# A four-layer graph network on one core: f1's first rows stored and spread through other queues, the decoder's last product in two parts

## The chip, the cores and the metric

One core of one Trainium2 chip runs the whole program in one launch. The metric is the device time of a launch in microseconds; the kernel before was run four times. Profiled executions are recorded by the hardware profiler, which gives every instruction's start and duration on TensorE (PE, and PEld for its weight loads), VectorE (DVE), ScalarE (ACT), GpSimd (POOL) and SyncE (SP), and the DMA traffic by queue: q1 is fed by SP, q10 by ACT, q0 by GpSimd.

## The reference

Input are 2708 nodes with 512 features (x) and a 2708 x 2708 adjacency matrix of zeros and ones (adj, about 1.2% ones and the diagonal). Four layers follow, each as `x = layernorm(x + layer(x, adj))`:

```
layer 0:  Xw = x @ W (4 heads of 128);  f1 = Xw . v1,  f2 = Xw . v2
          att = softmax over the neighbours of sigmoid(f1[i] + f2[j])
          Xa = att @ Xw;  batchnorm;  emb = batchnorm(elu(Xn @ We.T + b) + Xn)
          Y = elu((att @ emb) @ W.T);  out = batchnorm(elu(Y @ Wd.T + b) + Y)
layer 1:  A @ (x @ W + b) / degree
layer 2:  adj * (softmax(x @ node_w) * softmax(masked (x Ew)(x Ew).T)) @ (x W) + b
layer 3:  softmax(q k.T / sqrt(512) + 2 adj) @ v
```

The change lies in layer 0: at its very start, where f1 is made, and at the end of its decoder (the last line of layer 0), where the statistics of the last batchnorm are completed.

## The kernel before

The 2708 nodes are cut into 22 row blocks of 128 (the last has 20 rows). Layer 0 works on two halves of the columns (1354 each, a half being three chunks of 452, 452 and 450) and two pairs of heads. Features lie on the partitions in "feature tiles" of 128 x 4 x 2708, called xT_sb, ft and ot in turn.

**The start (project, L219 to L323).** SP's queue loads x transposed in six chunks (L232), and in between the first two blocks of the adjacency (L241), small weights and the parameters (L243). PE makes f1 for a chunk (f1_rows, L263: four products of 32 rows each), DVE copies it to the tile `stage` (L270). After the three chunks of the first half, one DMA of 4 x 1354 floats stores f1 to DRAM (L275), and two DMAs read one head's row each and spread it to 128 partitions (L277): f1b[0] and f1b[1], 677 KB each. They are needed because f1 has to lie along the free axis on every partition. All three DMAs are issued by SP. Beside this, PE makes Xw and f2 for the 22 row blocks (values_of, L285, three PSUM tiles in turn), ACT copies Xw of the first 14 blocks to SBUF and DVE that of the others (L294), and DVE takes f2 (L298).

**The attention pass (attention_pass, form).** For each row block j, the adjacency block is loaded (L379, by SP), zeros become a large negative number (DVE, L395 and L396), and the block is stored to adj_d for later passes (L400, by GpSimd). ACT computes tanh(0.5 f1 + 0.5 f2) for both heads (L407, from f1b[0] and f1b[1]), DVE combines it with the mask (L415, 128 x 2708), ACT takes the exponential (L416), and PE adds the block's share to the output sums (L503, twelve records a block) and to the row sums (L540). Four tiles t and four tiles a are in flight. The loads of blocks 2 and 3 are ordered behind the second spread where that is an instruction of their own queue (issue_after, which orders instructions of one engine).

**What sets the order.** A scheduler writes one instruction order for each engine from the program's order, dependencies and its own estimates; an engine then runs its list in order. A DMA's wait stands in the list of the engine that issues it, so whatever is behind it on that engine waits too.

**The decoder's end (decode, from L862).** For the last pair of heads of the second half, three chunks q are taken in turn. For each chunk and each of four groups o of 128 features, mlp makes one product (L914, four matmuls of 128 x 128 weights with 452 or 450 columns, two records each), ACT the exponential (L558), DVE the two steps of the elu (L563, L565), the sum with the input (L938) and the batch statistics (L939, bn_stats). Of the last chunk's last group, o = 3, everything after it depends: bn_aggr (L575) over six partial statistics for each o, scale and shift (L107 to L109, L578, L585, L586), and then layer 1's input stage, in which ACT applies scale and shift (L1066), DVE adds x (L1073) and PE transposes (L1079) and multiplies with w1 (L128). Beside the tail, PE makes one small product for a later layer (L1020), ACT copies it (L1027), and SP stores it (L1028).

Of the kernel before, what the change touches and what calls it, by code (L numbers as in the profile page):

```python
# [29 lines left out]
def gnn_stack_kernel(  # L30
# [25 lines left out]
    nc = tc.nc  # L56
    N, F = x.shape
    H = w0.shape[1]
    C = F // P
# [75 lines left out]
    NHALF, HB, HP = 2, 3, 2  # L135
# [10 lines left out]
    SQ = 4  # L146
# [31 lines left out]
    with ExitStack() as l0:  # L178
# [8 lines left out]
        f1_d = dram.tile([H, N], F32, name="f1_d")  # L187
# [6 lines left out]
        def feat_tile(name):  # L194
            return pf.tile([P, C, N], F32, tag="feat", name=name)
# [23 lines left out]
        def project(att, psum):  # L219
# [39 lines left out]
            def f1_rows(ci, dst):  # L259
                c0, w = CHUNKS[ci]  # L260
                pf = psum.tile([P, BANK], F32, tag=f"psm{ci % 2}", name="pf")
                for h in range(H):
                    nc.tensor.matmul(  # L263
                        pf[32 * h : 32 * h + 32, :w],
                        wv1[:, h, :],
                        xT_sb[:, h, c0 : c0 + w],
                        start=True,
                        stop=True,
                    )
                nc.vector.tensor_copy(dst[:, :w], pf[:, :w])  # L270

            h0, w = HSPAN[0]
            for ci, (q0, _) in enumerate(HCH[0]):
                f1_rows(ci, stage[:, q0:])
            nc.sync.dma_start(f1_d[:, h0 : h0 + w], stage[0 : 32 * H : 32, :w])  # L275
            for k in range(HP):
                spread = nc.sync.dma_start(  # L277
                    f1b[k][:, :w], f1_d[k, h0 : h0 + w].partition_broadcast(P)
                )
            def values_of(jt):  # L280
# [287 lines left out]
        def stats_tile(name, k):  # L568
            return p0.tile([P, C, k, 6], F32, tag=name, name=name)

        def batch_scale(stats, gamma, name):

            mv = pf.tile([P, C, 2], F32, name=f"{name}_mv")
            for c in range(C):
                nc.vector.bn_aggr(mv[:, c, :], stats[:, c].rearrange("p k s -> p (k s)"))  # L575
            scale = pf.tile([P, C], F32, name=f"{name}_scale")
            inv_std(scale, mv[:, :, 1], BN_EPS)
            nc.vector.tensor_tensor(scale, scale, prm_sb[:, gamma, :], ALU.mult)  # L578
            return scale, mv[:, :, 0]
# [27 lines left out]
        stats = stats_tile("stats_a", SQ * NHALF)  # L607
        bias = p0.tile([P, 2, C], F32, name="enc_bias")
        with (
# [3 lines left out]
            f1b, blocks, spread, rest = project(att, psum)  # L613
# [84 lines left out]
            for name, w in (("wq", wq), ("wk", wk)):  # L698
                for part in range(2):
                    tag = "z" if len(raws) == 3 else "a"  # L700
                    t = att.tile([P, HW], F32, tag=tag, name=name, bufs=1 if tag == "z" else 4)
                    t = t[:, : half * F].rearrange("p (c o) -> p c o", c=half)
# [19 lines left out]
        with (  # L722
# [41 lines left out]
            stats = stats_tile("stats_b", NCH)  # L764
# [16 lines left out]
            for ci, (c0, w) in enumerate(CHUNKS):  # L781
# [15 lines left out]
                for o in range(C):  # L797
                    dst = ft[:, o, c0 : c0 + w]
                    r = elu(
                        att, pss[o][:, :w], w, bias[:, 0, o : o + 1], bias[:, 1, o : o + 1]  # L800
                    )
# [16 lines left out]


            ot = feat_tile("ot")  # L820
            stats = stats_tile("stats_c", NCH)
            dec_w = load_mlp(dec_wT, "dec_w")
            links = {}
            spare = []
# [37 lines left out]
            def decode(hf, p, po, rb):  # L862
                h0, w = HSPAN[hf]
# [8 lines left out]
                t = ot[:, :, h0 : h0 + w]  # L872
                last = p + 1 == H // HP
                final = last and hf == NHALF - 1
# [30 lines left out]
                    nc.tensor.matmul(ps[:, :qw], w0T_sb[:, h, :], y, start=True, stop=True)  # L905
                    elu(att, ps[:, :qw], qw, dst=y)

                def mlp(q, o, st, wide):


                    q0, qw = HCH[hf][q]
                    ps = psum.tile([P, BANK], F32, tag="misc", name="ps_dec", bufs=2)
                    for c in range(C):
                        last_dec[0] = nc.tensor.matmul(  # L914
                            ps[:, :qw],
                            dec_w[:, c, o * P : (o + 1) * P],
                            t[:, c, q0 : q0 + qw],
                            start=(c == 0),
                            stop=(c == C - 1),
                        )  # L920
                    r = None
                    if wide:
                        if o == 0:
                            st["r"] = att.tile([P, HP, HW], F32, tag="t", name="r_dec", bufs=4)
                        r = st["r"].rearrange("p k w -> p (k w)")[:, o * BW : o * BW + qw]
                    r = elu(
                        att,
                        ps[:, :qw],
                        qw,
                        prm_sb[:, MB_DEC, o : o + 1],  # L930
                        bm1[:, o : o + 1],
                        dst=r,
                        last=final and q + 1 == HB and o + 1 == C,
                    )
                    st.setdefault("sums", []).append((t[:, o, q0 : q0 + qw], r, o))

                    def add(dst, y, r, o):
                        nc.vector.tensor_tensor(dst, y, r, ALU.add)  # L938
                        nc.vector.bn_stats(stats[:, o, HB * hf + q, :], dst)  # L939

                    if wide and o + 1 < C:
                        y, r, o = st["sums"][-1]
                        add(r, y, r, o)
                    elif o + 1 == C:
                        for y, r, o in st["sums"]:
                            if wide and o + 1 < C:
                                nc.scalar.copy(y, r)
                            else:
                                add(y, y, r, o)

                def after(k, q):
                    shifted(k, q)
# [2 lines left out]
                if not final:  # L955
# [4 lines left out]
                    for q in range(HB if last else 0):  # L960
                        st = {}
                        wide = q + 1 == HB
# [25 lines left out]
                for q in range(HB):  # L988
                    st = {}
                    mlp(q, 0, st, True)  # L990
                    mlp(q, 1, st, True)
                    if q + 1 < HB:
                        turns(q + 1)
                    if q + 2 < HB:
                        begin(q + 2)
                    mlp(q, 2, st, True)
                    if q == 0:
                        centre(po[0])
                    mlp(q, 3, st, True)


                rest = [
# [32 lines left out]
        nc.vector.tensor_reduce(dsum, zeros, AX.X, ALU.add)  # L1035
        nc.vector.tensor_scalar(dsum, dsum, -1.0, float(N), ALU.mult, ALU.add)
        nc.vector.reciprocal(rdeg, dsum)
        scale3, mean3 = batch_scale(stats, MG_DEC, "bn3")
        shift3 = batch_shift(scale3, mean3, MBETA_DEC, "bn3")
        xs, w1_sb, x_held = held1["xs"], held1["w1"], held1["x"]  # L1040

# [2 lines left out]
    with (  # L1044
# [62 lines left out]
        for g in range(0, NT, G):  # L1107
            group = range(g, min(g + G, NT))
            c0 = g * P
            w = min(N, c0 + G * P) - c0  # L1110
# [35 lines left out]
            for it in group:  # L1146
                n = BLOCKS[it][1]
                y = xs[:n, it, :]
# [412 lines left out]
    with (  # L1561
# [61 lines left out]
    with (  # L1623
# [96 lines left out]
        def finish3(it, po, rs):  # L1720
# [23 lines left out]
            sums=lambda: room(13, 4, C, GW),  # L1744
# [9 lines left out]
        for t in range(start3 + steps + lag):  # L1754
# [87 lines left out]
```

## Time and profile before

| | us |
|---|---|
| median of four runs | 3234.18 (3232.56 to 3238.33) |
| the profiled execution's own time | 3238.33 |
| its span | 3236.6 |
| PE busy | 3200.6 (99%) |
| DVE busy | 1929.2 (60%) |
| ACT busy | 1318.8 (41%) |
| f1 rows ready on DVE (L270's third copy ends) | 19.12 |
| first spread, second spread issued by SP | 24.62, 24.96 |
| first tanh, second tanh start | 30.79, 33.48 |
| first L503 on PE | 44.08 |
| last product of the decoder ends on PE, about | 1152.9 |
| last bn_aggr ends on DVE | 1157.08 |
| first transpose of layer 1 on PE | 1159.23 |

The span is the time from the first to the last instruction of the profiled execution; a little of the launch lies around it. PE's busy time is modelled from the starts of pipelined matmuls, so it says where PE stands still, not how well it is used. A gap on PE is read with its "granted clock", the TensorE clock that was in force, as a share of full speed. In a timeline row the numbers are the start, the length, the engine, the line and what it writes and reads; the bracket at the end is the idle time of the engine before it, and who ended it.

### The profile page before, as it was taken

Reading aid. Unit: us, or ns where it says so; the run is one execution under the profiler, and the core shown is the slowest. Engines: PE = TensorE matmul, PEld = TensorE weight load, DVE = VectorE, ACT = ScalarE, POOL = GpSimd, SP = SyncE. Lnnn points to the kernel's source line nnn. Section 1 sums busy time; section 2 is a strip of 40 time slices with the busy share of each in tenths; the row PEclk is TensorE's granted clock in tenths of the full one; section 3 lists DMA queues with packets and bytes.
Section 4 is the critical chain, followed back from the end, with each engine's and each line's share of the span. In section 5 each row is a group of like instructions: output and inputs, shape, how many; then the busy total and the mean of one; then the engine's idle time right before and its main releaser. Section 6 shows DMA issues by size and latency. Waiting matters only on the chain.

```text
span 3236.6 us, 30335 instructions
## 1 busy us (share of the span) xinstructions
PE 3200.6 (99%) x10874; PEld 1716.2 (53%) x10874; DVE 1929.2 (60%) x3160; ACT 1318.8 (41%) x1498; POOL 136.3 (4%) x220
## 2 busy tenths in 40 slices
PE   8999999999999999999999999999999999999999
PEld 5444444544444446875555555554555555555554
DVE  7889987876686685444145677776344342542533
ACT  6898886467767451001143434442011020120211
POOL 1100100000000000000010000000000000000000
PEclk9999999999999999999999999999999999999999
DMA  8867865256555413540054444553211111111100
GB/s 281 313 221 265 290 236 188 71 170 231 189 172 187 166 57 116 144 115 1 1 147 121 130 128 137 149 160 98 75 41 34 43 35 38 43 30 46 34 24 20
DMA packets 175702, 400.35 MB, mean 124 GB/s; under 512 B 21275, under 2 KB 116455, under 8 KB 169215
## 3 DMA queue, kind: packets, MB, share of 16 engines
q1 hardware_dynamic: 158622, 315.64, 32.0%
q0 software_dynamic: 16496, 80.70, 6.5%
q8 instruction: 85, 1.39, 0.2%
q10 hardware_dynamic: 432, 2.08, 0.2%
q14 instruction: 67, 0.54, 0.0%
HBM read 315.46 MB, written 81.30 MB: 123 GB/s over the span
## 4 chain that ended last, share of the span: by engine, by line
PE 85%; issue 8%; DVE 3%; ACT 2%; DMA 1%; POOL 1%; SPq 0%; POOLq 0%; DVEq 0%; ACTq 0%
PE po L1407 24%; PE ps_s L1286 18%; PE po L503 16%; PE ps_nb L1139 7%; PE ps_wide L1188 5%; PE ps_sup L1584 2%; PE ps_hid L128 2%; PE ps_o L1515 2%; PE ps_dec L914 2%; PE ps_mlp L789 1%; PE psm L540 1%; PE ps_s L1278 1%; ACT t L416 1%; PE tp L1178 1%; DVE t L415 1%
## 5 line engine op out<-in xcount | busy, mean ns | idle before, releaser
L415 DVE SCALAR_TENSOR_TENSOR t<-t,a 128x2708 f32<-128x2708 f32 (+1 forms) x150 | 444.3, 2975 | 151.8 <-ACT t L407 147.7
L407 ACT ACTIVATE t<-f1b,f2h 128x1354 f32<-128x1354 f32 (+1 forms) x300 | 411.6, 1413 | 59.1 <-PE po L503 32.9
L503 PE MATMUL po<-t,xw 128*128 128x452 f32 (+3 forms) x1056 | 410.5, 552 | 4.2 <-ACT t L416 4.2
L1286 PE MATMUL ps_s<-sup,hT 128*128 128x384 f32 (+1 forms) x1176 | 407.4, 490 | 0.0
L1407 PE MATMUL po<-sup,e 128*128 128x512 f32 x882 | 407.0, 595 | 0.0
L1407 PE MATMUL po<-e,xs 128*128 128x384 f32 (+1 forms) x1176 | 406.0, 489 | 0.0
L416 ACT ACTIVATE t<-t 128x2708 f32<-128x2708 f32 (+1 forms) x150 | 367.9, 2454 | 90.7 <-DVE t L415 90.6
L503 PE MATMUL po<-t,emb 128*128 128x452 f32 (+3 forms) x1056 | 398.5, 546 | 3.8 <-ACT t L416 3.8
L1718 DVE SCALAR_TENSOR_TENSOR e<-a_cols,ps_s 128x384 f32<-128x384 f32 (+1 forms) x154 | 85.5, 555 | 449.9 <-PE ps_s L1286 427.0
L1286 PEld LDWEIGHTS ps_s<-sup,hT 128*128 128x128 f32 x1176 | 221.8, 190 | 164.2 <-issue 14.2
L1407 PEld LDWEIGHTS po<-e,xs 128*128 128x128 f32 x1176 | 222.2, 190 | 160.2 <-issue 5.8
L503 PEld LDWEIGHTS po<-t,xw 128*128 128x128 f32 (+1 forms) x1056 | 189.9, 191 | 213.8 <-issue 198.2
L503 PEld LDWEIGHTS po<-t,emb 128*128 128x128 f32 (+1 forms) x1056 | 194.2, 191 | 201.1 <-issue 193.2
L1407 PEld LDWEIGHTS po<-sup,e 128*128 128x128 f32 x882 | 160.4, 190 | 159.3 <-issue 137.1
L1286 PE MATMUL ps_s<-hT 128*128 128x384 f32 (+5 forms) x672 | 211.0, 461 | 0.9 <-ACT sup L1591 0.7
L1385 ACT ACTIVATE e<-e 128x384 f32<-128x384 f32 (+1 forms) x308 | 151.7, 522 | 117.4 <-DVE e L1384 114.6
L1139 PE MATMUL ps_nb<-hid_hi,at 128*128 128x512 f32 x484 | 185.4, 390 | 0.4 <-DVE at L1131 0.4
L1633 ACT ACTIVATE a_cols<-a_cols,neg_big 128x384 f32<-128x384 f32 (+1 forms) x154 | 94.6, 617 | 217.9 <-DMA a_cols<-in_adjT_dram 185.6
L1139 PE MATMUL ps_nb<-hid_lo,at 128*128 128x512 f32 x462 | 179.9, 389 | 0.0
L1384 DVE TENSOR_TENSOR e<-e,nmax 128x384 f32<-128x384 f32 (+1 forms) x308 | 162.6, 550 | 23.3 <-ACT nmax L1377 23.3
L108 ACT ACTIVATE ln_rstd<-ln_rstd 128x1 f32<-128x1 f32 (+1 forms) x88 | 17.3, 201 | 388.8 <-DVE ln_rstd L107 388.0
L1286 PEld LDWEIGHTS ps_s<-hT 128*128 128x128 f32 x672 | 123.2, 190 | 89.3 <-issue 19.6
(253 smaller groups left out, 3323.4 us busy)
## 6 DMA issues: line engine op xcount, KB each, us to landing
a<-adj_d SPq DMA_DIRECT2D x108, 677.0 KB
a_cols<-in_adjT_dram SPq DMA_DIRECT2D x378, 192.0 KB
kept<-t POOLq DMA_DIRECT2D x22, 1354.0 KB, 6.4
t<-kept SPq DMA_DIRECT2D x22, 1354.0 KB
a<-in_adjT_dram SPq DMA_DIRECT2D x42, 677.0 KB
adj_d<-a POOLq DMA_DIRECT2D x42, 677.0 KB, 6.1
raw<-in_adjT_dram SPq DMA_DIRECT2D x105, 256.0 KB
a_cols<-in_adjT_dram SPq DMA_DIRECT2D x63, 202.0 KB
```

Source lines behind the costliest of these rows:

```text
L407: tanh = nc.scalar.activation(tv[:, k, :], f1b[k][:n, :w], AF.Tanh, bias=f2h[:n, jt, h : h + 1], scale=0.5,)
L415: step = nc.vector.scalar_tensor_tensor(tv, tv, GUARD, ab, ALU.add, ALU.mult)
L416: exp = nc.scalar.activation(tv, tv, AF.Exp, scale=0.5)
L503: nc.tensor.matmul(po[HB * k + q][:, :qw], values[r : r + n, jt, h * P : (h + 1) * P], t[r : r + n, k, q0 : q0 + qw], start=(place == 0), ...
L1139: nc.tensor.matmul(pos[it][:n], at, half[:, jt, :], start=(jt == 0 and k == 0), stop=(jt == NT - 1),)
L1188: nc.tensor.matmul(ps[:, :width], w(c, o), xt(c), start=(c == 0), stop=(c == C - 1),)
L1286: nc.tensor.matmul(ps[:, b * P : w], keys[:, c, j0 : j0 + P], st["q"][:, c, b * P :], start=(c == 0), stop=(c == C - 1),)
L1384: nc.vector.tensor_tensor(e, e, st["nmax"][:, :w], ALU.add)
L1385: nc.scalar.activation(e, e, AF.Exp)
L1407: nc.tensor.matmul(out, lhsT, rhs, start=(k == 0), stop=(k == NT - 1))
L1633: nc.scalar.activation(a, a, AF.Identity, bias=neg_big[: a.shape[0]], scale=1.0e30)
L1718: nc.vector.scalar_tensor_tensor(e, a, 2.0, ps, ALU.mult, ALU.add)
```

## The change

Three edits. The store of f1's first rows is issued by ACT instead of SP. The spread of the second head's row is issued by GpSimd instead of SP. The last product of the decoder (last chunk, o = 3) is computed in two parts of 225 columns, each with its own exponential, elu, sum and statistics; the statistics tile has one more place for it (and takes the storage of an earlier one), and bn_aggr of o = 3 runs over seven places, of the others over six as before.

```diff
-            nc.sync.dma_start(f1_d[:, h0 : h0 + w], stage[0 : 32 * H : 32, :w])
+            nc.scalar.dma_start(f1_d[:, h0 : h0 + w], stage[0 : 32 * H : 32, :w])
             for k in range(HP):
-                spread = nc.sync.dma_start(
+                queue = nc.gpsimd if k else nc.sync
+                spread = queue.dma_start(
                     f1b[k][:, :w], f1_d[k, h0 : h0 + w].partition_broadcast(P)
                 )
...
-        def batch_scale(stats, gamma, name):
+        def batch_scale(stats, gamma, name, more=0):
...
             for c in range(C):
-                nc.vector.bn_aggr(mv[:, c, :], stats[:, c].rearrange("p k s -> p (k s)"))
+                k = stats.shape[2] - (more if c + 1 < C else 0)
+                nc.vector.bn_aggr(mv[:, c, :], stats[:, c, :k].rearrange("p k s -> p (k s)"))
...
-            stats = stats_tile("stats_c", NCH)
+            stats = stats_tile("stats_a", SQ * NHALF)[:, :, : NCH + 1]
...
-                def mlp(q, o, st, wide):
+                def mlp(q, o, st, wide, part=None):
                     q0, qw = HCH[hf][q]
+                    nth = HB * hf + q
+                    if part is not None:
+                        q0, qw, nth = q0 + part * (qw // 2), qw // 2, nth + part
+                    done = part in (None, 1)
...
-                        last=final and q + 1 == HB and o + 1 == C,
+                        last=final and q + 1 == HB and o + 1 == C and done,
...
-                    st.setdefault("sums", []).append((t[:, o, q0 : q0 + qw], r, o))
+                    st.setdefault("sums", []).append((t[:, o, q0 : q0 + qw], r, o, nth))
...
-                    if wide and o + 1 < C:
+                    if not done:
+                        y, r, o, nth = st["sums"].pop()
+                        add(y, y, r, o, nth)
+                    elif wide and o + 1 < C:
...
-                    mlp(q, 3, st, True)
+                    if q + 1 < HB:
+                        mlp(q, 3, st, True)
+                    else:
+                        mlp(q, 3, st, True, 0)
+                        mlp(q, 3, st, True, 1)
...
-        scale3, mean3 = batch_scale(stats, MG_DEC, "bn3")
+        scale3, mean3 = batch_scale(stats, MG_DEC, "bn3", more=1)
```

The engines' orders move with it. On ACT the store stands behind the fifth of the 14 copies of Xw. On GpSimd the second spread stands behind the first adj_d store. On DVE the mask step L395 of block 2 stands ahead of the first L415 (before, behind the copy of the last f1 chunk, L270), and some mask steps near the end of the first half change places with L415. At the decoder's end DVE interleaves the two parts of o = 3 with the steps of o = 2; on ACT the three copies of r_dec (L947) stand between the two exponentials, and the square root of the scale (L108) ahead of the copy L1027.

More of the change, by code (lines that the diff above doesn't have):

```diff
@@ L924, in mlp @@
                             st["r"] = att.tile([P, HP, HW], F32, tag="t", name="r_dec", bufs=4)
-                        r = st["r"].rearrange("p k w -> p (k w)")[:, o * BW : o * BW + qw]
+                        r = st["r"].rearrange("p k w -> p (k w)")
+                        r = r[:, o * BW + (part or 0) * qw :][:, :qw]
                     r = elu(
@@ L932, in mlp, with add @@
                         dst=r,
-                        last=final and q + 1 == HB and o + 1 == C,
+                        last=final and q + 1 == HB and o + 1 == C and done,
                     )
-                    st.setdefault("sums", []).append((t[:, o, q0 : q0 + qw], r, o))
-                    def add(dst, y, r, o):
+                    st.setdefault("sums", []).append((t[:, o, q0 : q0 + qw], r, o, nth))
+                    def add(dst, y, r, o, nth):
                         nc.vector.tensor_tensor(dst, y, r, ALU.add)
-                        nc.vector.bn_stats(stats[:, o, HB * hf + q, :], dst)
-                    if wide and o + 1 < C:
-                        y, r, o = st["sums"][-1]
-                        add(r, y, r, o)
+                        nc.vector.bn_stats(stats[:, o, nth, :], dst)
+                    if not done:
+                        y, r, o, nth = st["sums"].pop()
+                        add(y, y, r, o, nth)
+                    elif wide and o + 1 < C:
+                        y, r, o, nth = st["sums"][-1]
+                        add(r, y, r, o, nth)
                     elif o + 1 == C:
-                        for y, r, o in st["sums"]:
+                        for y, r, o, nth in st["sums"]:
                             if wide and o + 1 < C:
@@ L948, in mlp @@
                             else:
-                                add(y, y, r, o)
+                                add(y, y, r, o, nth)
                 def after(k, q):
```

## The prediction

> **What bounds the kernel now.** I read the page's summary first: PE is busy 99% of the span and is 85% of the chain that ended last, so an edit counts only where PE stands still or where something moves PE's start. The change touches two such places, the first 50 us and the end of the decoder, about 1150 to 1160 us. For the first I read the chain of waits over the first 60 us (start, length, what):
>
> ```profile
> 18.48 0.64 DVE f_rows L270
> ...
> 19.14 5.46 DMA f_d<-f_rows
> ...
> 25.01 8.45 DMA f1b<-f_d
> ...
> 33.48 1.43 ACT t L407
> ...
> 34.93 2.98 DVE t L415
> ...
> 38.73 2.09 PE pxw L285 x8
> ```
>
> The f1 rows are ready at 19.12, their store takes until 24.60, the two spreads until 33.48 (the first head's row lands at 30.79). The first mask step (L415) runs 34.93 to 37.91, and PE, which had run out of work at 35.54, waits until 38.73, because the copies that free its PSUM tiles (L294 on DVE) stand behind that step in DVE's order. The windows view shows what the wait costs beyond itself (after the window: busy us and count of PE, PEld, DVE, ACT, POOL, then granted clock, DMA share, GB/s):
>
> ```profile
> 36.00:38.00 2.00, 0.00 (x0) 0.00 (x0) 2.00 (x2) 1.58 (x3) 0.00 (x0) 0.99 0.76 311
> 38.00:40.00 2.00, 1.27 (x6) 1.30 (x7) 2.00 (x7) 2.00 (x1) 0.00 (x0) 0.50 0.52 84
> 40.00:42.00 2.00, 2.00 (x10) 1.42 (x10) 1.61 (x4) 2.00 (x3) 0.62 (x1) 0.50 0.68 274
> 42.00:44.00 2.00, 2.00 (x12) 0.55 (x9) 2.00 (x3) 1.04 (x1) 0.57 (x1) 0.50 0.05 9
> 44.00:46.00 2.00, 2.00 (x5) 1.07 (x5) 2.00 (x4) 0.87 (x1) 0.02 (x1) 0.81 0.20 44
> ```
>
> After the gap of 3.19 us the clock is 0.50 to about 45 us. The same view shows a second case: PE waits 3.31 us before 864.73 and has 0.50 until about 870. The third gap is the decoder's end, 2.79 us up to 1159.23, and there the clock stays:
>
> ```profile
> 1156.40:1159.30 2.90, 0.12 (x2) 0.08 (x2) 1.80 (x9) 1.75 (x5) 0.00 (x0) 1.00 0.63 175
> ```
>
> So between 2.79 and 3.19 us of idle lies a step, and the start is just past it. From 50.43 on PE starts a new row block every 6.03 us (50.43, 56.46, 62.48) without a gap, DVE needs 5.5 per block; what the start gains or loses, the end gains or loses.
>
> At the decoder's end the timeline shows DVE, not PE, as the last:
>
> ```profile
> 1153.98 0.69 DVE L563 TENSOR_SCALAR elu_r<-ps_dec,bm 128x450 f32<-128x450 f32 x1 [0.21 <-ACT elu_m L558]
> 1154.70 0.63 DVE L565 SCALAR_TENSOR_TENSOR r_dec<-elu_m,elu_r 128x450 f32<-128x450 f32 x1
> 1155.43 0.63 DVE L938 TENSOR_TENSOR ot<-ot,r_dec 128x450 f32<-128x450 f32 x1
> 1156.10 0.63 DVE L939 BATCH_NORM_STATS2 stats_c<-ot 128x6 f32<-128x450 f32 x1
> 1156.76 0.32 DVE L575 BATCH_NORM_AGGREGATE bn_mv<-stats_c 128x2 f32<-128x36 f32 x1
> ```
>
> The 0.21 is DVE's only wait since 1150.75; scale and shift follow, and PE's first transpose comes at 1159.23.
>
> **The store on ScalarE's queue.** SP's queue holds 7 MB of loads ahead of the store; the DMA share is 0.9 or more until 24 us. On ACT the store stands behind the fifth of the 14 copies of xw (19.10 to 19.69), so it starts 0.55 later than SP's, costs 0.35 of ACT (the L453 issues take 326 to 348 ns), and nine copies and then the tanh steps are queued behind it. ACT idles 0.31 before each of these copies, which hides it; without that cover it is 0.35 on the PSUM copies. Landing: the nearest rows are the three 7 KB stores to the same tensor from GpSimd's queue, 1.7, 3.2 and 4.9 us. From 19.69 that is 21.4 to 24.6; I take the middle, 22.9. The first spread on SP then starts 1.7 earlier (0 to 3.2).
>
> **The second spread on GpSimd's queue.** In the built order it stands behind the first adj_d store (L400), which waits for DVE's L396 and runs 24.36 to 25.07. So it is issued at 25.1, no earlier than now (25.0). The early store alone cannot bring it forward; the gain must come from not lying behind the first spread in one queue. Against that, it lies behind a store of the same 677 KB, and the loads of row blocks 2 and 3 (SP) no longer stand behind it but compete. Its price is bounded by the same queue's 677 KB stores (view of tile a, first 120 us):
>
> ```profile
> DMA to landing us min/median/max: 4.1/5.4/9.6
> ```
>
> Added to 25.1: 29.2, 30.5, 34.7, against 33.48 now. The two stores issued beside the heavy loads (24.36 and 29.93) took 8.0 and 8.1, which gives 33.2. I take 7.0, between the median and these: 32.1, a gain of 1.4. A rule speaks against the edit: the Trainium skill, DMA: Bandwidth & Descriptors, "Issuing engines are not separate DMA queues", says that all issuers run on the same 16 DMA engines and interleave, so that another issuer saves only sequencer time. By that rule the second row would land as now, and this part of the sum would be zero. The rows here show the DMA engines nearly idle, 58 GB/s, from 24 to 26 us, between the loads' end and the first spread; an earlier first spread can fill that hole, so I do not take the rule's zero.
>
> **What moves with it.** In the new order DVE's L395 of block 2 (0.86) stands ahead of the first L415. Its load now follows the first spread directly, so I expect it in time; if not, the load's wait lands on L415. GpSimd's second adj_d store is not held (GpSimd idles 4.86 before it). SP has two issues less.
>
> **PE after the gap.** With the second row 1.4 earlier, L415 runs 33.5 to 36.5, and PE resumes at 37.3 instead of 38.73. The idle time shrinks to 1.8, below the 2.79 that kept the clock, so PE stays at 1.00. The rest of the projections (16 records at 0.12, eight f1 records, 0.96) then takes 2.9 instead of 5.35, to 40.2, where L503 starts instead of 44.08. Its first 8 records end at 43.3; the last four wait for the copy of block 21 behind the second L415 (ended 45.68, now 1.6 earlier, 44.1), then 1.6 and the row sums 1.28: 47.0 against 50.43. The exponentials keep up: the third one (ended 54.24, now about 52) is needed at 53.0. I take 3.3. The clock's share of this is weighed once more: the Trainium skill, TensorE: Matmul & The Clock Gate, "What's actually happening", puts the step at about 3.4 us of a free-running window, so a gap above 1.7 can sit on either side of it by phase. By it a long gap might pass unthrottled, and only the 1.4 would be left.
>
> **The decoder in two parts.** DVE durations by width: 292 ns at 128, 480 at 324, 505 at 340, 628 at 450, so 1.04 ns an element and about 393 at 225; one start to the next is 0.67 at 450 and by that 0.43 at 225, 0.72 and 0.49 for L563. The last product's four steps cost 0.72 + 3 x 0.67 = 2.73 now and 2 x (0.49 + 3 x 0.43) = 3.56 in halves: 0.83 more, on an engine without gaps; the 0.21 wait is filled. Sum: 0.6 longer. The bounds: if DVE were free when the second half arrives, PE's end (1153.1, 16 records at 0.197 against 8 at 0.384) plus 0.1, an exponential of 0.45, 0.49, 3 x 0.43 and 0.35 gives 1155.8 against 1157.08, so 1.3 shorter; if the second exponential, now behind three copies on ACT, is late as well, 0.83 + 0.45 = 1.3 longer. I take 0.6, as DVE is full. ACT's copy of mqk (L1027) moves behind the square root, some 1.6 later, and with it SP's store, the last x piece and the b1 row (issued 1159.73); its user comes at 1164.86, so this is nothing. The statistics tile only changes its storage.
>
> **Sum.** 0.6 - 3.3 = -2.7. The profiled execution took 3238.33 (span 3236.6), 4.15 above the median of the four runs, 3234.18; it would come to 3235.6, the median to **3231.5**.
>
> **Rivals.**
> - *The row lands early* (the median of 5.4 us, at 30.5). PE hardly waits; L503's last records follow the second L415, 3.3 earlier: 42.4 + 1.6 + 1.28 = 45.3, so 5.1 gained, with 0.6 lost: 3229.7. For it: GpSimd's queue may be served in turn with SP's. Against: 8.0 beside loads.
> - *Hidden anyway*: the row lands as now, 33.5, PE's gap and half clock stay, the decoder's 0.6 is left: 3234.8.
> - *Slower, GpSimd's queue late*: the row takes 9.6 behind the adj_d store and lands at 34.7. PE waits 4.4, the clock falls all the same, everything is 1.2 later, with 0.6: 3236.0. It decides from 8.4 us of issue to landing on.
>
> **How the numbers follow.** Forecast 0.42, early 0.27, hidden 0.12, late 0.12, things that I don't see 0.07. A measurement can tell about 0.2%, 6.5 us. Faster than that needs the early row and the decoder's best end (5.1 + 1.3): half of its case and 0.01 of the rest, 0.15. Slower by it needs a row at 39 us or later: a quarter of the late case and most of the rest, 0.09. Within: 0.76. The range runs from the early case with the decoder's best end, 3227.8, less the runs' scatter of about 1.5 to the late one with the decoder's worst, 3236.7, and the same scatter: 3226.5 to 3238.
>
> **What would show it.** The first f1 store landed by 23; the first tanh by 29; the second tanh at 33.5 minus the gain; PE's gap under 2.8 and 1.00 from 38 to 45; the first row sums ended near 47; the last bn_aggr 0.6 later after PE's last product. I am wrong if the half clock stays, if the second row lands after 33.5, or if DVE finishes the halves sooner.

## The result, and the profile after

The changed kernel takes 3238.09 us (median of 41 runs) against 3233.98 (61 runs of the kernel before): a ratio of 1.0011, 95% interval 1.0006 to 1.0015, so 3.6 us more (1.9 to 4.9; the medians themselves lie 4.1 apart). That is within 0.2%, but slower where 3231.5, 2.7 us faster, was forecast, and just above the range of 3226.5 to 3238. The profiled execution took 3238.37 (span 3236.6), as long as that of before, which lay 4 us above its median: the two traces are compared stage by stage, not end to end.

The chain of waits over the first 60 us, of the changed kernel (start, length, what), answers to the one of before:

```profile
22.95 1.49 DVE a L398
...
24.74 0.71 POOL adj_d L402
25.45 11.13 DMA f1b<-f_d
...
36.60 1.43 ACT t L409
...
38.05 2.98 DVE t L417
...
41.85 2.08 PE pxw L287 x8
```

The store of the f1 rows is no longer in the chain. In its place stands GpSimd's queue: the mask step, the first adj_d store, and behind it the second spread, which takes 11.13 us from its issue to its landing. The first head's tanh could start at 29.18 (30.79 before), but the second waits until 36.60 (33.48 before). PE's gap grows from 3.19 to 5.91 us. The windows of the changed kernel, with the columns of those of before:

```profile
36.00:38.00 2.00, 0.00 (x0) 0.00 (x0) 0.00 (x0) 1.40 (x2) 0.00 (x0) 1.00 0.62 251
38.00:40.00 2.00, 0.00 (x0) 0.00 (x0) 1.95 (x1) 2.00 (x3) 0.00 (x0) 0.72 0.00 0
40.00:42.00 2.00, 0.15 (x1) 0.18 (x2) 2.00 (x4) 1.58 (x2) 0.00 (x0) 0.50 0.00 0
42.00:44.00 2.00, 2.00 (x9) 1.76 (x10) 1.61 (x6) 2.00 (x2) 0.14 (x1) 0.50 0.93 276
44.00:46.00 2.00, 2.00 (x15) 1.34 (x14) 2.00 (x5) 2.00 (x2) 0.94 (x2) 0.57 0.19 74
```

PE stands still through the first two windows and nearly the third, and then works at half clock until 45.7. The first row sums start at 51.23 rather than 49.15.

The decoder's end went the other way. DVE's rows in the timeline of the changed kernel:

```profile
1151.18 0.45 DVE L565 TENSOR_SCALAR elu_r<-ps_dec,bm 128x225 f32<-128x225 f32 x1
1151.55 0.62 DVE L949 TENSOR_TENSOR r_dec<-ot,r_dec 128x450 f32<-128x450 f32 x1
1152.08 0.39 DVE L567 SCALAR_TENSOR_TENSOR r_dec<-elu_m,elu_r 128x225 f32<-128x225 f32 x1
...
1154.40 0.35 DVE L949 TENSOR_TENSOR ot<-ot,r_dec 128x225 f32<-128x225 f32 x1
1154.79 0.40 DVE L950 BATCH_NORM_STATS2 stats_a<-ot 128x6 f32<-128x225 f32 x1
1155.22 0.34 DVE L579 BATCH_NORM_AGGREGATE bn_mv<-stats_a 128x2 f32<-128x42 f32 x1
```

The first three belong to two different products, and each starts before the one ahead of it has ended: 0.37 after a step of 0.45 us, 0.53 after one of 0.62. The last three depend on each other and start 0.39 and 0.43 apart. The first transpose comes 5.3 us after the decoder's last product ends on PE (1152.38 to 1157.71), against 6.2 before. But the windows of 3.41 us that end and begin at 1158.45 show what follows:

```profile
1155.04:1158.45 3.41, 1.50 (x5) 0.50 (x4) 2.20 (x10) 2.30 (x7) 0.00 (x0) 1.00 0.67 216
1158.45:1161.86 3.41, 3.41 (x8) 1.65 (x7) 2.75 (x9) 3.18 (x8) 0.53 (x1) 0.50 0.91 294
```

After a gap of only 1.91 us the clock is at 0.50 for one such window; after 2.79 us it was not, in the trace of before.

### The profile page after: what moved, and what is told of

Same layout as the page of the kernel before. It is cut to its first block, busy times and chain, and to the rows that moved or that the text cites. A ratio compares the mean times of both kernels' runs of the same rounds, so it can differ in the third digit from the quotient of the medians.

```text
span 3236.6 us, 30356 instructions
## 1 busy us (share of the span) xinstructions
PE 3200.2 (99%) x10882; PEld 1718.0 (53%) x10882; DVE 1928.5 (60%) x3164; ACT 1319.1 (41%) x1499; POOL 136.1 (4%) x221
## 3 DMA queue, kind: packets, MB, share of 16 engines
q8 instruction: 85, 1.39, 0.2%
## 4 chain that ended last, share of the span: by engine, by line
PE 84%; issue 9%; DVE 3%; ACT 2%; DMA 1%; POOL 1%; SPq 0%; POOLq 0%; DVEq 0%; ACTq 0%
PE po L1425 24%; PE ps_s L1304 18%; PE po L505 16%; PE ps_nb L1157 7%; PE ps_wide L1206 5%; PE ps_hid L128 2%; PE ps_sup L1602 2%; PE ps_o L1533 2%; PE ps_dec L924 2%; PE ps_mlp L793 1%; PE psm L542 1%; PE ps_s L1296 1%; ACT t L418 1%; PE tp L1196 1%; ACT t L409 1%
## 5 line engine op out<-in xcount | busy, mean ns | idle before, releaser
L1304 PEld LDWEIGHTS ps_s<-sup,hT 128*128 128x128 f32 x1176 | 221.8, 190 | 164.2 <-issue 14.2
L108 ACT ACTIVATE ln_rstd<-ln_rstd 128x1 f32<-128x1 f32 (+1 forms) x88 | 17.3, 202 | 390.5 <-DVE ln_rstd L107 389.8
```

The costliest lines, as they stand in the source:

```text
L1304: nc.tensor.matmul(ps[:, b * P : w], keys[:, c, j0 : j0 + P], st["q"][:, c, b * P :], start=(c == 0), stop=(c == C - 1),)
```

## The experiments

**The marks.** Runs of one kernel lie from 3 us below to 7 above their median (61 runs of before), as much as the effects, so each run's trace is read at marks as well. The loads at the start vary, and with them the moment when the f1 rows are ready (17.9 to 19.5); so the row's time and the ninth row sums (after which PE goes on every 6.03 us) are also given from that moment. "Halves" is the decoder's last product in two parts, "spread" the second head's row issued by GpSimd. The column "half" is the stretch at granted clock 0.50 after the gap. Each row is one trace; ratios are to runs of the kernel before beside it.

| kernel | rows ready | second tanh, after rows | PE gap | half | ninth row sums, after rows | ratio (95%) |
|---|---|---|---|---|---|---|
| before, first trace | 19.11 | 33.48, 14.4 | 3.19 | 6.83 | 97.37, 78.3 | |
| before, second trace | 18.75 | 32.68, 13.9 | 2.76 | 6.83 | 96.61, 77.9 | |
| halves alone | 18.37 | 32.56, 14.2 | 3.01 | none | 94.41, 76.0 | 0.9998 (0.9989 to 1.0007) |
| store alone | 18.74 | 31.27, 12.5 | 1.36 | none | 93.12, 74.4 | 0.9997 (0.9989 to 1.0006) |
| spread alone | 18.56 | 37.74, 19.2 | 7.99 | 6.83 | 100.67, 82.1 | 1.0024 (1.0013 to 1.0034) |
| changed kernel | 19.50 | 36.60, 17.1 | 5.91 | 6.83 | 99.45, 80.0 | 1.0011 (1.0006 to 1.0015) |
| no spread | 18.85 | 31.61, 12.8 | 1.59 | none | 93.46, 74.6 | 0.9989 (0.9981 to 0.9998) |
| no spread, repeated | 17.95 | 30.86, 12.9 | 1.74 | none | 92.71, 74.8 | 0.9992 (0.9984 to 1.0001) |
| no spread, end filled | 19.26 | 31.56, 12.3 | 1.14 | none | 93.42, 74.2 | 0.9987 (0.9979 to 0.9996) |
| loads behind spread | 18.74 | 32.46, 13.7 | 2.54 | 3.41 | 95.03, 76.3 | 0.9993 (0.9984 to 1.0002) |
| spread first | 19.09 | 33.52, 14.4 | 3.25 | 6.83 | 97.48, 78.4 | 1.0000 (0.9989 to 1.0010) |
| start filled | 19.37 | 36.33, 17.0 | 0.64 | none | 98.07, 78.7 | 1.0007 (0.9998 to 1.0016) |

**One edit alone, three times.** The store alone:

```diff
-            nc.sync.dma_start(f1_d[:, h0 : h0 + w], stage[0 : 32 * H : 32, :w])
+            nc.scalar.dma_start(f1_d[:, h0 : h0 + w], stage[0 : 32 * H : 32, :w])
```

> The kernel before with one edit: f1's first rows are stored from ScalarE's queue; both spreads stay on SyncE's, the decoder's last product stays whole. Theory (the second row, spread by GpSimd's queue, is the whole loss): in the trace of the changed kernel this store landed only as the loads in SyncE's queue ran out, 0.27 us earlier than before, so here both spreads come 0 to 0.4 earlier, the second tanh starts between 33.1 and 33.5, the PE gap stays at about 3 us with the clock at 0.50 behind it, and the time is 0 to 0.5 us shorter: no difference that can be measured. Rival A (the store is the loss: it holds ScalarE for 1.06 us, and the rows were ready 0.38 later): the second tanh comes after 33.8 and the time is 1 to 3 us longer.

Measured: the second tanh at 31.27, earlier than the theory had it; the gap 1.36, the clock 1.00; the time not told from before (1.0 us less; 3.6 less to 1.9 more). Rival A falls: the ScalarE issue does take 1.06 us, but the second head's row is 1.6 earlier, counted from the moment when the f1 rows are ready.

The spread alone:

```diff
-                spread = nc.sync.dma_start(
+                queue = nc.gpsimd if k else nc.sync
+                copy = queue.dma_start(
...
+                spread = spread if k else copy
```

> The kernel before with one edit: the second head's row is spread by GpSimd's queue (the loads of blocks 2 and 3 stay ordered behind the first spread, as in the changed kernel); the store stays on SyncE's queue, the decoder's last product stays whole. Theory (this edit is the whole loss of the start): it is issued behind the first adj_d store and lands 9 to 11 us after its issue, at 34.5 to 37; the second tanh starts 2 to 3 us later than 33.48, the PE gap grows from 3.2 to over 5, the first row sums come about 2 later than 49.15, and the time is 2 us longer (1 to 3.5). Rival A (the store is the loss): second tanh by 33.8, no longer than before. Rival B (the halves of the decoder are the loss): start later or not, time within 1 of before.

Measured: 7.8 us longer (4.2 to 11), more than the theory's 3.5. In this build the spread stands behind the second adj_d store as well: it is issued at 29.91 and lands 7.8 later. So the size isn't the changed kernel's, the direction is; rivals A and B fall.

The halves alone (the two hunks of the start undone):

> The kernel before with one edit: the decoder's last product in two parts; the start is that of before. Theory (clock): from the end of the exponential of o = 2 of the last chunk to PE's first transpose it takes 8.5 us rather than 9.15, so 0.6 is gained there; if the clock falls to 0.50 after the transposes as in the changed kernel, 1.5 is lost again, and the time is 0.9 longer; if it does not fall, 0.6 shorter. Either way within 1.5 of before. Rival B (the halves are the loss): 2 to 4 us longer. The step as forecast (DVE has no room): 0.6 later at the first transpose.

Measured: the first transpose 5.34 us after the product, half clock for 3.41 us behind it (1152.58 to 1155.99), the time not told from before (3.6 us less to 2.3 more). "0.6 later" falls. Rival B has no more than the edge of this interval, and falls with the next kernel, which has the halves and is faster than before.

**The changed kernel without the spread**, and the same again later:

```diff
-                queue = nc.gpsimd if k else nc.sync
-                spread = queue.dma_start(
+                spread = nc.sync.dma_start(
```

> The changed kernel with the second spread back on SyncE's queue; the store on ScalarE's queue and the two parts of the decoder's product stay. Theory (the spread is the whole loss): the second tanh starts at 31 to 32 as with the store alone (31.27), the PE gap is below 2 us, the clock stays 1.00 until 50 us, the row sums come at 45 to 46.5, and the time is 3 to 6 us below the changed kernel's, 0 to 2.5 below before. Rival (store and halves are neutral one by one, but together with another order of the instructions they cost): the time stays 2 or more above before.

> The changed kernel without the GpSimd spread once more (its first comparison gave 3.6 us less than before, interval 0.6 to 6.1): beside the kernel with the filled gap on the same chip, and to see whether it stays below before. Theory: again 1 to 5 us below before; the second tanh at 31 to 32; if the half clock follows the transposes in this execution, it lasts 3.41 us. Rival (the first result was chance): within 1 of before.

Measured: 3.6 us below before (0.6 to 6.1), more than the 0 to 2.5 of the theory; the second time 2.6 (-0.3 to 5.2), which by itself doesn't exclude zero. The chain of the first of them:

```profile
18.90 4.72 DMA f_d<-f_rows
...
24.03 7.56 DMA f1b<-f_d
31.61 1.43 ACT t L408
33.07 2.98 DVE t L416
```

The store is back in the chain, 4.72 long, and the second spread behind the first takes 7.56, both through SyncE's queue. Undoing this one edit turns the result round.

**Why the row is late: two experiments.** The loads behind the spread:

```diff
                         loads.append(
-                            nc.sync.dma_start(a[:n, :w], src[j0 : j0 + n, h0 : h0 + w])
+                            (nc.gpsimd if early else nc.sync).dma_start(
+                                a[:n, :w], src[j0 : j0 + n, h0 : h0 + w]
+                            )
                         )
```

> The changed kernel, with the loads of adjacency blocks 2 and 3 issued by GpSimd's queue behind the second spread instead of by SyncE's, so that they can't run beside it. Theory K (competition: the loads, no longer ordered behind the second spread, take half of the DMA engines from it): the second row lands at 31 to 33.5 rather than 36.6, the PE gap falls below 3.2, the time is 2 to 5 us below the changed kernel's. Theory Q (queue: the row lies behind the first adj_d store, and GpSimd's queue moves its first data some 5 us after the issue, loads or not): the row lands at 35 or later, and the time is that of the changed kernel.

The spread first in its queue:

```diff
-                    nc.gpsimd.dma_start(adj_d[j0 : j0 + m, h0 : h0 + w], a[:m, :w])
+                    early = hf == 0 and jt < len(blocks)
+                    with tc.issue_after(spread.ins) if early else nullcontext():
+                        nc.gpsimd.dma_start(adj_d[j0 : j0 + m, h0 : h0 + w], a[:m, :w])
```

> The changed kernel, with the adj_d stores of blocks 0 and 1 ordered behind the second spread on GpSimd, so that the spread is first in its queue; the loads of blocks 2 and 3 stay on SyncE's queue beside it. Theory Q (queue): the spread is issued when the store has landed, at 24 to 24.5, its data moves from 28 to 29, and the second tanh starts at 31.5 to 33.5; the time is 2 to 5 us below the changed kernel's. Theory K (competition): it lands at 34.5 or later, and the time is at most 2 below the changed kernel's.

Measured: 13.7 and 14.4 us after the rows, instead of 17.1. On SyncE's queue it is 12.6, so each of the two takes more than half of the lateness away, and the two overlap: both theories hold in part, and neither alone. The DMA view, by queue (packets, MB, share of the 16 engines), first the changed kernel from 30 to 34 us:

```profile
q1 hardware_dynamic: 170, 0.83, 50.3%
q0 software_dynamic: 165, 0.81, 48.6%
```

then with the loads behind the spread, from 28 to 30 us:

```profile
q0 software_dynamic: 138, 0.66, 102.7%
```

Where SyncE's queue (q1) has loads, GpSimd's (q0) gets half; where it has none, all. The beginning differs too. In the changed kernel q0's first data moved about 5 us after the first issue in it (24.74 to between 29.5 and 30). With the loads behind the spread, q1 had only the first spread left, and q0's first packet moved 2 to 2.5 us after the issue (23.98 to between 26 and 26.5), the bulk from 27 on. In the kernel with the spread alone q1 moved nothing from 25 to 27, and q0's first store began 1.2 to 1.7 us after its issue (23.81 to between 25 and 25.5). The Trainium skill says that DMAs from different issuers run on the same 16 engines and interleave (DMA: Bandwidth & Descriptors, "Issuing engines are not separate DMA queues"): the 50.3% and 48.6% show just that. Even in the best of the three orders the row is later than the 12.3 to 12.9 of SyncE's queue.

**Less ahead of the store.** Two kernels, from the one before, issue loads behind the spreads instead of ahead of the store: x's last chunk and adjacency block 1, or the chunk alone.

```diff
...
+            with tc.issue_after(spread.ins):
+                nc.sync.dma_start(blocks[1][:, :w], adjT[P : 2 * P, :w])
+                c0, w = CHUNKS[NCH - 1]
+                spread = nc.sync.dma_start(
+                    xT_sb[:, :, c0 : c0 + w],
+                    xT[:, c0 : c0 + w].rearrange("(c p) j -> p c j", p=P),
+                )
```

> The kernel before, with SyncE's loads of adjacency block 1 and of x's last chunk (1.6 MB together) issued behind the two spreads instead of ahead of the store; store and spreads stay on SyncE's queue, the decoder's product stays whole. Theory (what holds the store, and with it the spreads, is the bytes queued ahead of it on the DMA engines, whichever queue issues it): the store lands by 21.5 rather than 24.6, the second tanh starts at about 30.2 rather than 33.5, and the row sums come 2 to 4 earlier than 49.15, unless the mask steps of block 1, now later on DVE, hold PE's copies; the time is 1 to 4 us shorter. Rival C (the store has a latency of its own of some 5 us, whatever is queued): it lands at 24 or later, the second tanh starts after 33, and the time is the same or longer, as x's last chunk comes later.

> The kernel before, with SyncE's load of x's last chunk (0.92 MB) issued behind the two spreads; everything else as before, the load of adjacency block 1 among it. With adjacency block 1 moved as well, the store landed 2.2 us after its issue, the second tanh started at about 29.4, but the mask steps of block 1 then stood ahead of the copies that free PE's tiles. Theory (bytes queued ahead of the store hold it): the store lands 3 to 4 us after its issue rather than 5.5 to 6.3, the second tanh starts at 30.5 to 31.5, the PE gap is below 2, the clock stays 1.00, row sums at 43.5 to 46, the time 1 to 4 us below before. Rival (a wait elsewhere takes it: x's last chunk is late for the last projections, or layer 1's bias row, which in the trace of before lands just as it is needed, holds the gain): row sums earlier, but the time the same within 1.

Measured: the first spread is issued 2.2 and 4.4 us after the rows are ready (5.5 to 6.4 in the four traces with the store on SyncE's queue behind all loads), and the second tanh starts at 29.25 and 29.55. So the bytes ahead hold the store, as the theory says, and rival C falls. But the times are 1.0003 (0.9994 to 1.0012) and 0.9993 (0.9984 to 1.0002), not told from before. PE now stops at 31.7. Its rows where it goes on, first with both loads behind, then with the chunk alone:

```profile
33.48 2.92 PE L294 MATMUL pxw<-held,xT_sb 128*128 128x130 f32 x24 [1.74 <-DMA xT_sb<-in_xT_dram]
38.12 1.13 PE L294 MATMUL pxw<-held,xT_sb 128*128 128x130 f32 x8 [1.71 <-DVE f2h L307]
```

```profile
35.35 4.01 PE L292 MATMUL pxw<-held,xT_sb 128*128 128x130 f32 x19 [3.69 <-DMA xT_sb<-in_xT_dram]
```

PE waits for x's last chunk, the very load that was put behind the spreads: 1.74 and 3.69 us. The further 1.71 is a wait for DVE's copies, which in that kernel stand behind the mask steps of block 1 (34.84 to 37.30). The ninth row sums come 76.4 and 77.6 after the rows, within the 76.0 to 78.3 of the three traces with the start of before. The rival of the second kernel (x's last chunk is late for the last projections) holds: the wait has moved. That the row is early is not enough; what was put behind it has to be in time as well.

**The clock.** The kernel before, traced again:

> The kernel before, unchanged, for a second trace of its start: the first one had the clock at 0.50 after a PE gap of 3.19 us and took 4.2 us longer than the median. Theory (the window's phase decides): the second tanh starts between 32.3 and 33.6, the PE gap is 2.9 to 3.3 us; if more than about 1.85 us of it lie in one window of 3.41 us, the clock falls for 3.41 or 6.83 us and the row sums of the ninth block come near 97; if the gap is split more evenly, it stays and they come near 94.4. Rival (a fixed threshold between 2.79 and 3.19 us of idle, as forecast): a gap above 3.19 lowers the clock, one below 3.01 doesn't, wherever the windows lie.

It took 3241.12, with a PE gap of 2.76 us. The windows that lie on the edges of its half clock, then those of the halves alone:

```profile
33.80:37.21 3.41, 1.38 (x13) 0.44 (x11) 3.07 (x2) 2.99 (x4) 0.00 (x0) 1.00 0.97 403
37.21:40.62 3.41, 2.69 (x12) 2.30 (x13) 3.02 (x8) 3.41 (x2) 0.62 (x1) 0.50 0.66 208
```

```profile
33.01:36.42 3.41, 1.79 (x16) 0.86 (x15) 2.40 (x1) 3.41 (x3) 0.00 (x0) 1.00 1.01 418
36.42:39.83 3.41, 2.02 (x20) 1.85 (x24) 3.41 (x9) 2.99 (x3) 0.00 (x1) 1.00 0.61 181
```

A gap of 2.76 us lowered the clock, one of 3.01 did not: the first left PE idle for 2.03 us of one window, the second was cut by an edge into 1.62 and 1.39. The fixed threshold falls. In all 14 traces the half clock begins and ends on a grid of 3.413 us, at another phase in each; from the first to the second half clock in the trace of before it is 95.0 steps. Of the gaps at the start and at the decoder's end, every window with 2.03 us of idle or more (11) was followed by 0.50; none with 1.80 or less was, unless the clock was down already; of six with 1.89 to 1.96, four were. Why these six differ stays open. The Trainium skill states such a window (TensorE: Matmul & The Clock Gate, "What's actually happening": 3413 ns, free-running), and the edges agree. But a window need not be idle for all of its 3.41 us: 2.03 us were enough.

The end filled, with the spread back on SyncE's queue:

```diff
+                    for _ in range(2):
+                        last_dec[0] = nc.tensor.matmul(
+                            po[0], wq_again[:, 0, :], wk_again[:, 0, :], start=True, stop=True
+                        )
                 nc.scalar.activation(mqk, po[1], AF.Copy, scale=qscale)
```

> The changed kernel without the GpSimd spread (both spreads on SyncE), with two products more on PE (four records of 0.45 us, written to a PSUM tile that nothing reads) behind the small product at the decoder's end, which fill the 1.91 us that PE waits for the first transpose. Theory (clock: a gap of 1.9 us lowers the clock where it fills more than half of one of the 3.41 us windows that the edges of the half clock lie on, as in four of six runs with the halves): the first transpose comes 5.3 us after the decoder's product as without the fill, the clock stays 1.00 from 1140 to 1175, and from the first transpose to the next block's it takes 3.93 us and not 5.62; then layer 1's bias row is waited for, 0.5 to 1 us, and the time is 0 to 1.2 us lower than without the fill. Rival (the half clock there has another cause, such as the start of a dense stage): it falls in spite of the fill.

(The count in it is wrong: of the five kernels with halves, three had the half clock by then; with the later ones it is four of the seven whose gap is not filled.) PE's timeline with the fill:

```profile
1153.65 1.88 PE L1045 MATMUL po<-wk_again,wq_again 128*128 128x512 f32 x4
1155.81 0.62 PE L1100 MATMUL tp_out<-ident,ot 128*128 128x128 f32 x2 [0.28 <-DVE ot L1094]
...
1159.92 0.60 PE L1100 MATMUL tp_out<-ident,ot 128*128 128x128 f32 x4
```

The gap is 0.28, the clock stays, and the second block follows 4.1 us after the first transpose, where it took 5.62 in the two traces of this kernel without the fill. But this says little of the clock. Counted on from this trace's own half clocks, an edge of the grid lies at 1154.57; without the fill, PE would have stood still from about 1153.8 to 1155.7 (3.4 to 5.3 us after the decoder's product, as in the other traces with halves), cut into some 0.75 and 1.15 us, and by the traces above the clock would have stayed. That the fill kept it is not shown. The rival (the start of a dense stage) falls by other traces: loads behind spread, spread first and start filled enter the same stage after the same gap of 1.90 us at full clock, and need 3.93 us. In the filled trace layer 1's bias row is late: DVE waits 1.31 us for it, and PE loses 0.8. The time is 4.2 us below before (1.3 to 6.8), the lowest ratio here; against the kernel without the fill the difference can't be told.

The start filled, on the changed kernel:

```diff
+            turn = [None]
...
-                    nc.tensor.matmul(
+                    turn[0] = nc.tensor.matmul(
...
+            with tc.issue_after(turn[0].ins):
+                warm = psum.tile([P, BANK], F32, tag="psm0", name="warm")
+                for _ in range(6):
+                    nc.tensor.matmul(warm, w0T_sb[:, 0, :], xT_sb[:, 0, :BANK], start=True, stop=True)
```

> The changed kernel with six products more on PE (5.4 us, written to a PSUM tile that nothing reads) between the projections of row blocks 16 and 17, so that PE's wait of 5.9 us for the second row shrinks to about 1.3 and the clock can stay. Theory (row and clock: the late row costs the start some 3 us, the half clock behind the gap 1.5 more): the second tanh stays at 36 to 37, the clock is 1.00 from 34 to 50, the first row sums come 1.2 to 1.7 earlier than 51.23 on the same row time, and the time is 0.5 to 2 us below the changed kernel's, still 1 to 4 above before. Rival (the half clock is the whole loss of the start): the time falls to that of before or below.

Measured: the row as late as ever (36.33), the clock 1.00, the ninth row sums 1.3 earlier from the rows on (78.7 against 80.0), and 2.3 us above before (-0.6 to 5.2). So of the 5.5 us that the start of the changed kernel loses against the kernels without the spread (80.0 against 74.5), the half clock is the smaller part, 1.3, and the row's lateness the larger.

## Why the prediction was wrong

**The step that failed** is the price of the second spread: "I take 7.0, between the median and these: 32.1, a gain of 1.4". It took 11.1 and landed at 36.6, a loss of 3.1 on the trace of before. It was issued when the forecast had it, 6.0 us after the rows (25.45 here, 25.1 there); the transfer itself was mis-sized. It lies even beyond the upper bound of 9.6: the stores that gave this bound are issued at least 5 us apart (24.36, 29.93, 49.27, 54.42 and so on), this transfer 0.7 us behind a store of equal size in its queue, with two loads of equal size beside it. The prediction named the loads ("no longer stand behind it but compete") and the store, and gave neither a price of its own. The experiments price them: from the rows to the second tanh it is 17.1 with both (17.0 in the trace with the start filled), 14.4 without the store ahead, 13.7 without the loads, 12.6 on SyncE's queue. The zero that the prediction weighed, the row landing as now, did not come either. The rival "GpSimd's queue late" was the nearest: it named the store ahead, but not the loads, and had 34.7 for 36.6.

**The store** was right in direction, and its size too small. It was to land 3.8 us after the rows (22.9); the first spread is issued 4.8 to 4.9 after them in all eight traces with the store on ScalarE's queue, 5.5 to 6.4 where SyncE stores behind all loads. On ScalarE it cost 1.06 us, not 0.35, and delayed one copy by 0.27; no loss of it shows. With both spreads on SyncE the second row comes 1.5 earlier (12.6 against 14.2), and what the prediction derived for PE from a row 1.4 earlier then holds nearly to the letter: gap 1.8 (1.36), clock 1.00, L503 first at 40.2 (39.34), first row sums ended at 47.0 (46.2) in the kernel with the store alone. So the chain of reasons from the row to PE was sound, and hung on the wrong edit; only the full clock came out by another rule than the one given.

**The clock.** "Between 2.79 and 3.19 us of idle lies a step" is refuted by 2.76 with and 3.01 without half clock. The prediction's second thought, that a gap above 1.7 us can fall on either side by the phase of a free-running window, is what the traces show; its sum didn't use it. The start of before loses its clock in two traces of three (the halves alone have the same start), so the mean of its ninth row sums is 77.4 after the rows. With the store on ScalarE and both spreads on SyncE it is 74.5 (four traces), a gain of 2.9.

**The decoder** was to be 0.6 longer; it is 0.9 shorter up to the first transpose (5.34 against 6.23, within 0.01 in every trace but the filled one). The mis-sized term is 0.49 and 0.43 from one half step's start to the next. That holds only for steps that depend on each other (0.39 and 0.43); the interleaved ones follow after 0.29 to 0.37, so the eight half steps take 2.75 and not 3.56 us, and those of o = 2, interleaved with them, 2.39 and not 2.70; the wait of 0.21 goes. The 0.9 lies within the prediction's own bound of 1.3 shorter. What then gives it back was not foreseen: the half clock, and the bias row. Of the row's issue the prediction said that "its user comes at 1164.86, so this is nothing"; but this user was waiting for it. DVE stood still for 0.48 us ahead of it in the trace of before, where the profile names no releaser, and in the other kernels that come to it at full clock 0.7 to 1.7 us; in three of these the profile names the row, as in spread first:

```profile
1160.10 0.75 DVE L1108 SCALAR_TENSOR_TENSOR full<-ps_hid,ln_rstd,b_sb 128x512 f32<-128x512 f32 x1 [1.15 <-DMA b_sb<-in_b_dram]
```

By the seventh block's transposes 0.7 us is left (29.9 after the product, mean of the seven traces with halves and no fill, 29.1 to 30.3, against 30.6, mean of six without, 29.7 to 31.2).

**The sum** by the marks: -2.9 for the store, +5.5 for the spread (80.0 against 74.5), -0.7 for the halves: 1.9 us slower, at the lower end of the interval measured. Without the spread it is -3.6, and -3.6 and -2.6 were measured. For the other kernels, too, such a sum lies inside the interval measured. These are sums of single traces or means of a few, and the runs bear out their parts less sharply than their total: the store alone was measured 1.0 shorter, with an interval that includes both zero and its 2.9. What the changed kernel loses beyond 1.9, if anything, stays open; so does why GpSimd's queue begins later while SyncE's has work. The change that its three edits promised is the one without the second.

## What to carry to other kernels

A transfer's price on another queue is not a duration from the nearest row: ask what is ahead of it in that queue, what runs beside it on the shared engines, and which order held only because both sat in one queue. A stall of PE is worth more or less by the phase of a window, so one trace shows one draw; read several before a threshold is named. When a step comes early, look for what waits next: here the load that had been put behind it, the copies behind the mask steps, and a bias row that had just been in time. And ask of an experiment that fills a stall whether the stall would have cost anything in that trace.

## What the runs showed of the hardware

- The half clock sits on a grid of 3.413 us; a gap of 1.91 us can lower the clock, one of 3.01 us need not. One such window costs about 1.7 us where PE is the bound (5.62 against 3.93 from the first transpose to the second block).
- Traces with more such windows took longer. The two of before hold six and seven of them ahead of the last microseconds and took 3238.33 and 3241.12, against a median of 3233.98; that of the halves alone holds two, and took 3232.62. That they make the scatter between executions fits this, and is not shown.
- Where SyncE's queue had loads, GpSimd's got 48.6% of the DMA engines; where it had none, all. GpSimd's first data moved 1.2 to 1.7 us after the issue with SyncE's queue idle, 2 to 2.5 (a single packet) with one spread in it, about 5 with a spread and two loads.
- A store of 22 KB landed 2.2 us after its issue where the loads ahead of it ran out 2 us after that issue, and 4.3 to 6.3 with 0.7 to 1.6 MB more of them ahead, from SyncE's queue or ScalarE's.
- At the decoder's end of the changed kernel, two DVE steps that do not depend on each other and wait for no other engine start 0.08 to 0.09 us closer than the first one's recorded length; dependent ones, here and before, 0.03 to 0.10 further apart than it.
